# A four-layer graph attention kernel: normalised rows transposed by DMA in 16-bit halves in place of TensorE

## The chip, the cores and the metric

The kernel runs on one core of a Trainium2 chip. The metric is the device time of one execution in microseconds (us). Before the change three runs gave 2533.28 to 2535.13 us, median 2533.68.

## The reference

Four layers work on x (16 batches, 1024 nodes, 256 features, float32) and one adjacency matrix (1024 x 1024). Each layer normalises, projects, forms attention weights between all pairs of nodes, takes the weighted mean of the projected rows, and adds it to x:

```
h = max(layernorm(x), 0)
q = h @ W                                   # layers 0, 2: four heads of 64; layers 1, 3: one head of 256
e = leaky_relu(q @ a_src [i] + q @ a_dst [j])   # slope 0.2, in layer 3 0.01
attn = softmax over j of (e where adj, else -inf)
x = x + elu(attn @ q)                       # layer 3: relu in place of elu
```

Layers 0, 1 and 3 mask by adj > 0, layer 2 by adj != 0. Everything is float32.

## The kernel before

**Steps.** A step is one layer of one batch, 64 in all. Four batches are in work at a time (`STREAMS`), and `order_of_steps` interleaves them so that, but for the first few and the last, four-head and one-head steps alternate. A one-head step comes three places after the four-head step of the same batch, whose result it normalises; a four-head step comes five places after the one-head step before it, or starts a new batch.

**The main loop.** A step's work on TensorE is eight groups, each followed by an eviction (`aggregate`, L367 to L394). In a four-head step a group is half a head, 64-column pieces of the weight matrix as stationary operand and 65 moving columns; in a one-head step a group is one block of 128 rows with 257 columns. The last column carries the softmax denominator. ScalarE copies each group from its PSUM bank to `y` (L394). There are four such banks, shared with the projections and transposes. VectorE makes the weight tiles w (L363), one of 128 x 1024 for each head and block of 128 nodes, 32 in a four-head and 8 in a one-head step, into 18 buffers (`WBUFS`). The factor g that they read is broadcast over the partitions by a DMA (L346) and copied to PSUM by ScalarE (L358).

**The end of a step** (`finish`, L400 to L447) runs during the first groups of the next step: VectorE takes the reciprocal (L415), GpSimd scales (L425), ScalarE takes the exponential (L431), VectorE forms the ELU (L437) and GpSimd adds to x (L438).

**Preparation of a step** (`preparation`, L226) runs two to three steps ahead and is cut into 21 pieces: statistics on VectorE for each half of the nodes (L238), ten small operations on GpSimd that make the inverse deviation and the shift (L265 to L277; once for each half in a one-head step, once for both in a four-head step), normalisation of a half on ScalarE in four instructions (L283), two `transpose` pieces a half (eight TensorE transposes of 128 x 128 into a bank for each pair of halves and feature blocks, four a piece, evicted with Relu into `hT`, L291 and L292), four `project` pieces a half (two accumulating products each, L302, evicted by ScalarE, L304; after the fourth, two exponentials, L310 and L312, and a product on GpSimd, L314), and the factors and rows for g (L320 to L330).

**Order.** Nothing is scheduled by a program: each engine works in the order in which the code issues. A tuple of 21 numbers for each kind of step (`FOUR`, `ONE`, `SOON`, ...) says after which group each piece is issued, counted from the start of the step two places earlier. In the usual alternation `FOUR` and `ONE` apply. Pieces of two steps that fall on the same group are issued in the order of the steps. All ordinary DMAs go through SyncE's queue, in order too.

Of the kernel before, what the change touches and what calls it, by code (L numbers as in the profile page):

```python
# [26 lines left out]
F32 = mybir.dt.float32  # L27
BF16 = mybir.dt.bfloat16
I32 = mybir.dt.int32
U8 = mybir.dt.uint8  # L30
AF = mybir.ActivationFunctionType
ALU = mybir.AluOpType
AX = mybir.AxisListType
# [2 lines left out]
P = 128  # L36
EPS = 1e-5
SHIFT = 60.0
STREAMS = 4
WBUFS = 18  # L40

# [1 line left out]

FOUR = (-8, -8, -5, -3, -2, -1, -1, 0, 0, 0, 0, 0, 0, 2, 2, 2, 2, 3, 8, 8, 10)
SHORT = (-4, -4, -4, -2, -2, -1, -1, 0, 0, 0, 0, 0, 0, 2, 2, 2, 2, 3, 8, 8, 10)
ONE = (2, 2, 2, 4, 4, 5, 5, 6, 6, 6, 6, 6, 6, 8, 8, 8, 8, 8, 10, 10, 12)  # L50
SOON = (0, 0, 0, 1, 2, 3, 3, 4, 4, 5, 5, 5, 5, 6, 6, 7, 7, 7, 8, 8, 10)
FIRST = (-4, -4, -4, -2, -0.9, -1, -1, -0.8, -0.8, -0.8, -0.8, 0, 0, 1, 1, 1, 1, 1, 2, 2, 4)
TIGHT = (4, 4, 4, 6, 6, 7, 7, 8, 8, 8, 8, 8, 8, 9, 9, 9, 9, 9, 10, 10, 12)
LATE = (0, 0, 0, 1, 1, 2, 2, 3, 3, 3, 3, 3, 3, 4, 4, 4, 4, 5, 6, 6, 8)


LAYERS = [
# [8 lines left out]
def kernel(ctx: ExitStack, tc: tile.TileContext, x, adj, ws, avs, out):  # L66
    nc = tc.nc
    B, N, F = x.shape
    C = N // P
    K = F // P  # L70
    HALF = C // 2
# [3 lines left out]
    ident = const.tile([P, P], F32, name="ident")  # L75
# [8 lines left out]

    masks = [const.tile([P, C, N], U8, name=f"mask{i}") for i in range(2)]
    wx = []
# [11 lines left out]
    prep = ctx.enter_context(tc.tile_pool(name="prep", bufs=2))  # L98
# [9 lines left out]
    xs = {}  # L108
    state = [dict() for _ in steps]

    def bank(*shape):
        t = ps.tile([P, 512], F32, name="bank")
        n = math.prod(shape)
        if len(shape) == 1:
            return t[:, 0:n]
        names = "abc"[:len(shape)]
        return t[:, 0:n].rearrange(f"p ({' '.join(names)}) -> p {' '.join(names)}",
                                   **dict(zip(names, shape)))

    def heads_of(t, H):  # L120


        return t[..., 0:F + H].rearrange("p c (h d) -> p c h d", h=H)
# [7 lines left out]
    def weight_columns(l):  # L131
# [13 lines left out]
        def spread():  # L145
# [38 lines left out]
    def mask_rows(c):  # L184
# [3 lines left out]
        def fetch_rows():  # L188
            st["raw"] = work.tile([P, N], I32, name="w", bufs=WBUFS)
            nc.sync.dma_start(out=st["raw"], in_=adj.rearrange("(p c) j -> p c j", p=P)[:, c])  # L190

        def sign():
            st["sgn"] = work.tile([P, 2, N], BF16, name="w", bufs=WBUFS)
            nc.vector.tensor_scalar(st["sgn"][:, 0], st["raw"], -1.0, 1.0, op0=ALU.max,
                                    op1=ALU.min)
# [18 lines left out]
        def nonzero():  # L214
            nc.scalar.activation(masks[1][:, :, c * P:(c + 1) * P], st["pm"], AF.Square)

# [9 lines left out]
    def preparation(n):  # L226

        b, l = steps[n]
        H, slope, _, _ = LAYERS[l]
        D = F // H  # L230
        st = state[n]

        def stats(half):
            if half == 0:
                st["bn"] = small.tile([P, C, 6], F32, name="bn")
            bn = st["bn"]
            for c in range(half * HALF, (half + 1) * HALF):
                nc.vector.bn_stats(bn[:, c, :], xs[b][:, c, :])  # L238
            q = slice(half * HALF, (half + 1) * HALF)
            if n == 0:  # L240
                if half == 1:
                    combine_end(slice(0, HALF), nc.vector)
                combine(q, nc.vector)
            elif H == 1:

                combine(q, nc.gpsimd)
                combine_end(q, nc.gpsimd)
# [29 lines left out]
            engine.tensor_scalar(shift, shift, -0.5, None, op0=ALU.mult)  # L277

        def normalise(half):
            xn = st["xn", half] = prep.tile([P, HALF, F], F32, name="xn")  # L280
            for q in range(HALF):
                c = half * HALF + q
                nc.scalar.activation(xn[:, q, :], xs[b][:, c, :], AF.Identity,  # L283
                                     bias=st["shift"][:, c:c + 1], scale=st["rstd"][:, c:c + 1])

        def transpose(half, k):
            if k == 0:
                st["hT", half] = prep.tile([P, K, HALF * P], F32, name="hT")
            pt = bank(HALF, P)
            for q in range(HALF):  # L290
                nc.tensor.transpose(pt[:, q, :], st["xn", half][:, q, k * P:(k + 1) * P], ident)  # L291
            nc.scalar.activation(st["hT", half][:, k, :], pt.rearrange("p q i -> p (q i)"),  # L292
                                 AF.Relu)

        def project(c):
            if c == 0:
# [4 lines left out]
            for k in range(K):  # L301
                nc.tensor.matmul(pw, lhsT=st["hT", half][:, k, q * P:(q + 1) * P],  # L302
                                 rhs=wx[l][:, k, :], start=(k == 0), stop=(k == K - 1))
            nc.scalar.activation(st["whx"][:, c, :], pw, AF.Copy)  # L304
            if q < HALF - 1:
# [3 lines left out]
            wh = heads_of(st["whx"], H)[:, s]  # L309
            nc.scalar.activation(st["rcol"][:, s], wh[:, :, :, D], AF.Exp, bias=rbias[l],  # L310
                                 scale=1.0 - slope)
# [11 lines left out]
        def rows():  # L323
# [6 lines left out]
            nc.sync.dma_start(out=st["grow"].rearrange("h c i -> c h i"), in_=gT)  # L330

        out = [lambda: stats(0), lambda: stats(1), combine_all, lambda: normalise(0), lambda: normalise(1)]
        for half in range(2):
            out += [lambda half=half, k=k: transpose(half, k) for k in range(K)]
            out += [lambda c=c: project(c) for c in range(half * HALF, (half + 1) * HALF)]
# [24 lines left out]
    def weights(n, h, jc):  # L360

        w = state[n]["w", h, jc] = work.tile([P, N], F32, name="w", bufs=WBUFS)
        nc.vector.scalar_tensor_tensor(w, state[n]["g", h], state[n]["rcol"][:, jc, h:h + 1],  # L363
# [113 lines left out]
    def plan(n):  # L477
        new = preparation(n)
        agenda.extend((at, n, piece, i == len(new) - 1) for i, (at, piece) in enumerate(new))
        agenda.sort(key=lambda a: a[:2])  # L480
# [11 lines left out]
    def emit_heads(i):  # L492

        while done["g"] <= min(i + C // 2, done["tiles"] + C, len(tiles) - 1):
            n, h, _ = tiles[done["g"]]
            if n >= done["prepared"]:
                break
            broadcast(n, h)
            done["g"] += C
            fetch_heads()  # L500
# [12 lines left out]
    last, agenda_of = {}, []  # L513
    for n, (b, l) in enumerate(steps):

        free = -99
        if b % STREAMS in last:
            over = last[b % STREAMS] + 1
            free = 8 * over + (8 if l == 0 else 2 if LAYERS[steps[over][1]][0] == 1 else 4)
        last[b % STREAMS] = n  # L520
        start = 8 * (n - 2)
        kind = ONE if LAYERS[l][0] == 1 else SOON if n < 5 else FOUR
        if kind is FOUR and free > start + kind[0]:
            kind = SHORT
        if kind is ONE and free > start + kind[0]:
            kind = TIGHT
        if free > start + kind[0]:
            kind = LATE
            start = max(free, agenda_of[-1][0] + 5, start - LATE[7])
        agenda_of.append([start + k for k in kind] if n > 1 else FIRST)  # L530
        if n > 2:

            assert agenda_of[n][7] >= 8 * (n - 2)
            was = agenda_of[n - 1]
            assert agenda_of[n][3] >= was[5] and agenda_of[n][4] >= was[11]
    ending = []
    later = {}
    with tc.manual_schedule():
# [12 lines left out]
        nc.vector.tensor_copy(identb, ident)  # L551
        layer[0][1]()
        first = [piece for _, piece in preparation(0)]

        order = (
# [28 lines left out]
        for n in range(len(steps)):  # L584
            for k, (h, i0, per) in enumerate(groups(n)):
# [8 lines left out]
                while ending and ending[0][0] <= k:  # L594
                    ending.pop(0)[1]()
                upto = min(done["tiles"] + (6 if per > 1 else 3), done["free"] + WBUFS)
                emit_heads(upto - 1)
# [42 lines left out]
```

## Time and profile before

| what | value |
|---|---|
| median of three runs | 2533.68 us |
| profiled span | 2536.3 us |
| L379, aggregation on TensorE | 36,864 instructions, 1903.4 us busy |
| L302, projections on TensorE | 2,048 instructions, 481.5 us busy |
| L291, transposes on TensorE | 1,024 instructions, 136.8 us busy |
| L292, their evictions on ScalarE | 256, mean 585 ns |
| L283, normalisation on ScalarE | 512, mean 590 ns |
| L363, weight tiles on VectorE | 1,280, mean 1273 ns |
| L346, broadcast of a row by DMA | 159 of 512 KB |
| mean DMA rate over the span | 51 GB/s |

Busy time is the sum of an engine's instructions; matmuls are pipelined and their ends are modelled, so that the busy times on TensorE overlap a little. The chain is the work that ended last, followed back from the last instruction to whatever released it at each step; its shares say what a saved microsecond may be worth. A line of the timeline gives start, length, engine, line, operation, what it writes and reads, shapes and count, and in brackets the idle time ahead of it with what ended that time. PEld is TensorE's weight load, SPq the instructions that issue DMAs on SyncE.

### The profile page before, as it was taken

To read this page: it belongs to the slowest core of one execution; us is meant where nothing else is said; L and a number is where in the kernel's file an instruction comes from. 1 tells how busy PE (TensorE), PEld (TensorE's weight loads), DVE (VectorE), ACT (ScalarE), POOL (GpSimd) and SP (SyncE) were. 2 spreads that over 40 slices of the span, in tenths; PEclk is the share of its full clock that TensorE was granted. 3 is DMA by queue.
4 is the path that set the end of the run, shared out by engine and by line. 5 is a ranking of instruction groups with operands and counts; after the bars stand their busy time and mean duration, and the time that the engine had idled before them with its cause. 6 is when DMAs were issued, how large, how long until landed. Compare 5 with 4: busy or idle time off the path is not lost.

```text
span 2536.3 us, 88187 instructions
## 1 busy us (share of the span) xinstructions
PE 2489.7 (98%) x40096; PEld 2254.8 (89%) x40096; DVE 2014.6 (79%) x2138; ACT 1128.9 (45%) x2501; POOL 1106.6 (44%) x1366
## 2 busy tenths in 40 slices
PE   7999999999999999999999999999999999999999
PEld 6888898999988999988899899999889899899888
DVE  8988487888877987877888778878779887787973
ACT  6344455443454444544334544444444345544341
POOL 3345455443244554444332545543443345454351
PEclk9999999999999999999999999999999999999999
DMA  4201001122111111011221111111112201011101
GB/s 175 70 11 44 20 34 42 37 77 77 44 64 48 44 44 32 23 60 52 77 77 44 44 35 44 44 35 53 60 52 77 77 11 43 36 43 44 53 18 59
DMA packets 36847, 128.48 MB, mean 51 GB/s; under 512 B 6262, under 2 KB 9078, under 8 KB 34552
## 3 DMA queue, kind: packets, MB, share of 16 engines
q1 hardware_dynamic: 36462, 122.84, 13.8%
q8 instruction: 314, 5.14, 0.8%
q14 instruction: 61, 0.50, 0.1%
q10 hardware_dynamic: 10, 0.00, 0.0%
HBM read 105.39 MB, written 17.43 MB: 48 GB/s over the span
## 4 chain that ended last, share of the span: by engine, by line
PE 87%; DVE 7%; POOL 3%; issue 2%; ACT 1%; DMA 0%; DVEq 0%; SPq 0%; POOLq 0%; ACTq 0%
PE bank L379 65%; PE bank L302 17%; DVE w L363 5%; PE bank L291 4%; ACT xn L283 1%; POOL x L438 1%; DVE bn L238 1%; POOL rstd L271 1%; DVE e L437 0%; PE bank L326 0%; DVE e L424 0%; DVE wx L158 0%; DVE mask L211 0%; POOL shift L277 0%; DVE e L157 0%
## 5 line engine op out<-in xcount | busy, mean ns | idle before, releaser
L379 PE MATMUL bank<-whx,w 128*64 128x65 f32 x36864 | 1903.4, 241 | 20.9 <-issue 10.3
L379 PEld LDWEIGHTS bank<-whx,w 128*64 128x64 f32 x36864 | 1741.9, 144 | 162.8 <-issue 20.9
L363 DVE SCALAR_TENSOR_TENSOR w<-g,rcol,mask 128x1024 f32<-128x1024 f32 x1280 | 1540.6, 1273 | 359.2 <-PE bank L379 318.1
L394 ACT ACTIVATE y<-bank 128x260 f32<-128x260 f32 (+1 forms) x504 | 194.3, 386 | 1091.0 <-PE bank L379 1091.0
L425 POOL TENSOR_TENSOR y<-y,r 128x1024 f32<-128x1024 f32 x126 | 261.4, 2084 | 588.5 <-DVE e L424 435.1
L314 POOL TENSOR_TENSOR whx<-whx 128x1024 f32<-128x1024 f32 x128 | 259.2, 2025 | 561.9 <-ACT whx L312 561.9
L302 PE MATMUL bank<-wx,hT 128*128 128x264 f32 (+1 forms) x2048 | 481.5, 388 | 4.4 <-ACT y L394 3.9
L302 PEld LDWEIGHTS bank<-wx,hT 128*128 128x128 f32 x2048 | 382.4, 190 | 74.1 <-ACT y L394 13.1
L438 POOL TENSOR_TENSOR x<-x,e 128x1024 f32<-128x1024 f32 x96 | 246.0, 2572 | 144.9 <-DVE e L437 144.9
L283 ACT ACTIVATE xn<-x,shift,rstd 128x256 f32<-128x256 f32 x512 | 264.7, 590 | 72.9 <-POOL shift L277 70.9
L304 ACT ACTIVATE whx<-bank 128x264 f32<-128x264 f32 (+1 forms) x512 | 189.3, 385 | 178.4 <-PE bank L302 178.1
L238 DVE BATCH_NORM_STATS2 bn<-x 128x6 f32<-128x256 f32 x512 | 175.9, 411 | 77.2 <-POOL x L438 74.2
L437 DVE SCALAR_TENSOR_TENSOR e<-e,y 128x1024 f32<-128x1024 f32 x96 | 156.1, 1644 | 31.9 <-ACT e L431 22.8
L358 ACT ACTIVATE g<-gs 128x1024 f32<-128x1024 f32 x159 | 162.5, 1022 | 10.6 <-DVE w L363 7.8
L291 PE MATMUL bank<-ident,xn 128*128 128x128 f32 x1024 | 136.8, 275 | 7.6 <-ACT xn L283 7.4
L291 PEld LDWEIGHTS bank<-ident,xn 128*128 128x128 f32 x1024 | 119.8, 142 | 24.6 <-ACT xn L283 11.3
L292 ACT ACTIVATE hT<-bank 128x512 f32<-128x512 f32 x256 | 136.9, 585 | 1.1 <-PE bank L291 1.0
L271 POOL TENSOR_TENSOR rstd<-rstd,neghalf 128x4 f32<-128x4 f32 (+1 forms) x97 | 120.2, 1239 | 14.8 <-DVE shift L272 7.4
L431 ACT ACTIVATE e<-e 128x1024 f32<-128x1024 f32 x96 | 100.7, 1049 | 2.0 <-POOL e L427 1.7
L424 DVE SCALAR_TENSOR_TENSOR e<-y,r 128x1024 f32<-128x1024 f32 x58 | 68.5, 1222 | 2.1
L440 DVE SCALAR_TENSOR_TENSOR x<-y,x 128x1024 f32<-128x1024 f32 x30 | 43.3, 1444 | 10.0 <-POOL y L425 10.0
L312 ACT ACTIVATE whx<-whx,nbias 128x16 f32<-128x16 f32 (+1 forms) x128 | 40.2, 314 | 4.2
(65 smaller groups left out, 441.5 us busy)
## 6 DMA issues: line engine op xcount, KB each, us to landing
gs<-grow SPq DMA_DIRECT2D x159, 512.0 KB
x<-in_x SPq DMA_DIRECT2D x15, 1024.0 KB
out<-x SPq DMA_DIRECT2D x30, 512.0 KB
w<-in_adj SPq DMA_DIRECT2D x8, 512.0 KB
x<-in_x SPq DMA_DIRECT2D x2, 512.0 KB
wx<-in_L_gnn_W SPq DMA_DIRECT2D x8, 128.0 KB
out<-x SPq DMA_DIRECT2D x8, 128.0 KB
grow<-gT SPq DMA_DIRECT2D x32, 16.0 KB
```

Of the source, the lines that this page charges most:

```text
L238: nc.vector.bn_stats(bn[:, c, :], xs[b][:, c, :])
L283: nc.scalar.activation(xn[:, q, :], xs[b][:, c, :], AF.Identity, bias=st["shift"][:, c:c + 1], scale=st["rstd"][:, c:c + 1])
L291: nc.tensor.transpose(pt[:, q, :], st["xn", half][:, q, k * P:(k + 1) * P], ident)
L302: nc.tensor.matmul(pw, lhsT=st["hT", half][:, k, q * P:(q + 1) * P], rhs=wx[l][:, k, :], start=(k == 0), stop=(k == K - 1))
L304: nc.scalar.activation(st["whx"][:, c, :], pw, AF.Copy)
L314: nc.gpsimd.tensor_tensor(wh[:, :, :, 0:D], wh[:, :, :, 0:D], wh[:, :, :, D:D + 1].to_broadcast([P, HALF, H, D]), op=ALU.mult)
L358: nc.scalar.activation(g, state[n]["gs", h], AF.Copy)
L363: nc.vector.scalar_tensor_tensor(w, state[n]["g", h], state[n]["rcol"][:, jc, h:h + 1], masks[LAYERS[steps[n][1]][3]][:, jc, :], op0=ALU.m ...
L379: nc.tensor.matmul(acc[o % P:o % P + cols, q, :], lhsT=st["w", h, jc][:, o:o + cols], rhs=st["whx"][:, jc, h * (D + 1):(h + 1) * (D + 1)], ...
L394: nc.scalar.activation(st["y"][:, i0:i0 + per, h, :], acc, AF.Copy)
L425: nc.gpsimd.tensor_tensor(yh, yh, rb, op=ALU.mult)
L438: nc.gpsimd.tensor_add(xh, xh, e)
```

## The change

From the third step on, the normalised rows are transposed by the DMA engines. [...]GpSimd copies the lower and the upper 16 bits of a half's rows into two contiguous planes (`split`), one DMA on SyncE's queue transposes the sixteen 128 x 128 blocks of both planes, and ScalarE interleaves the two planes again while copying them to `hT` (`merge`). The integers pass through unchanged. `split` takes the place of the first `transpose` piece of a half and `merge` that of the second. Relu is applied by the normalisation. The aim is to free TensorE of the transposes and PSUM of their banks.

The four arrays of this path (normalised rows, planes, transposed planes, `hT`) share five buffers of 4 KB a partition (`HBUFS`), and the weight tiles give one up (`WBUFS` 17). The tuples move: in `FOUR` both normalisations and the first split come after the last group of the step before, the second split one group later, the merges one group after each other behind those, and all eight projections after one and the same group, the fourth of a step, where they stood in two pieces; in `ONE` splits and merges are two groups apart, the first four projections move from group 7 to group 8 of the step, and the rows for g come one group later.

```diff
-WBUFS = 18
+WBUFS = 17
+HBUFS = 5
-FOUR = (-8, -8, -5, -3, -2, -1, -1, 0, 0, 0, 0, 0, 0, 2, 2, 2, 2, 3, 8, 8, 10)
-SHORT = (-4, -4, -4, -2, -2, -1, -1, 0, 0, 0, 0, 0, 0, 2, 2, 2, 2, 3, 8, 8, 10)
-ONE = (2, 2, 2, 4, 4, 5, 5, 6, 6, 6, 6, 6, 6, 8, 8, 8, 8, 8, 10, 10, 12)
-SOON = (0, 0, 0, 1, 2, 3, 3, 4, 4, 5, 5, 5, 5, 6, 6, 7, 7, 7, 8, 8, 10)
+FOUR = (-8, -8, -5, -1, -1, -1, 1, 3, 3, 3, 3, 0, 2, 3, 3, 3, 3, 4, 8, 8, 10)
+SHORT = (-4, -4, -4, -1, -1, -1, 1, 3, 3, 3, 3, 0, 2, 3, 3, 3, 3, 4, 8, 8, 10)
+ONE = (2, 2, 2, 4, 5, 4, 6, 7, 7, 7, 7, 5, 7, 8, 8, 8, 8, 8, 11, 11, 12)
+SOON = (0, 0, 0, 1, 2, 1, 3, 4, 4, 5, 5, 2, 5, 6, 6, 7, 7, 7, 8, 8, 10)
-TIGHT = (4, 4, 4, 6, 6, 7, 7, 8, 8, 8, 8, 8, 8, 9, 9, 9, 9, 9, 10, 10, 12)
-LATE = (0, 0, 0, 1, 1, 2, 2, 3, 3, 3, 3, 3, 3, 4, 4, 4, 4, 5, 6, 6, 8)
+TIGHT = (4, 4, 4, 5, 6, 5, 7, 8, 8, 8, 8, 6, 8, 9, 9, 9, 9, 9, 10, 10, 12)
+LATE = (0, 0, 0, 1, 2, 1, 3, 4, 4, 4, 4, 2, 4, 5, 5, 5, 5, 5, 6, 6, 8)
...
         def normalise(half):
-            xn = st["xn", half] = prep.tile([P, HALF, F], F32, name="xn")
+            xn = st["xn", half] = prep.tile([P, K, HALF, P], F32, name="rows", bufs=HBUFS)
             for q in range(HALF):
                 c = half * HALF + q
-                nc.scalar.activation(xn[:, q, :], xs[b][:, c, :], AF.Identity,
+                nc.scalar.activation(xn[:, :, q, :],
+                                     xs[b][:, c, :].rearrange("p (k i) -> p k i", k=K), AF.Relu,
                                      bias=st["shift"][:, c:c + 1], scale=st["rstd"][:, c:c + 1])
+        def split(half):
+            xn = st["xn", half].rearrange("p k q i -> p (k q i)").bitcast(U16)
+            bits = prep.tile([P, 2, K * HALF * P], U16, name="rows", bufs=HBUFS)
+            nc.gpsimd.tensor_copy(bits.rearrange("p s n -> p n s"),
+                                  xn.rearrange("p (n s) -> p n s", s=2))
+            st["turned", half] = prep.tile([P, 2, K * HALF, P], U16, name="rows", bufs=HBUFS)
+            nc.sync.dma_start_transpose(
+                out=st["turned", half].rearrange("p s n i -> p (s n) i"),
+                in_=bits.rearrange("p s n -> p (s n)"))
+        def merge(half):
+            st["hT", half] = prep.tile([P, K, HALF * P], F32, name="rows", bufs=HBUFS)
+            nc.scalar.activation(
+                st["hT", half].rearrange("p k i -> p (k i)").bitcast(U16).rearrange(
+                    "p (n s) -> p n s", s=2),
+                st["turned", half].rearrange("p s n i -> p (n i) s"), AF.Copy)
         def transpose(half, k):
+            if n > 1:
+                (merge if k else split)(half)
+                return
...
-            assert agenda_of[n][3] >= was[5] and agenda_of[n][4] >= was[11]
+            assert agenda_of[n][3] >= agenda_of[n - 1][12]
```

More of the change, by code (lines that the diff above doesn't have):

```diff
@@ L30 @@
 U8 = mybir.dt.uint8
+U16 = mybir.dt.uint16
 AF = mybir.ActivationFunctionType
@@ L279, in normalise @@
         def normalise(half):
-            xn = st["xn", half] = prep.tile([P, HALF, F], F32, name="xn")
+            xn = st["xn", half] = prep.tile([P, K, HALF, P], F32, name="rows", bufs=HBUFS)
             for q in range(HALF):
                 c = half * HALF + q
-                nc.scalar.activation(xn[:, q, :], xs[b][:, c, :], AF.Identity,
+                nc.scalar.activation(xn[:, :, q, :],
+                                     xs[b][:, c, :].rearrange("p (k i) -> p k i", k=K), AF.Relu,
                                      bias=st["shift"][:, c:c + 1], scale=st["rstd"][:, c:c + 1])
+        def split(half):
[13 more added lines that the diff above has]
+                st["turned", half].rearrange("p s n i -> p (n i) s"), AF.Copy)
         def transpose(half, k):
+            if n > 1:
+                (merge if k else split)(half)
+                return
             if k == 0:
-                st["hT", half] = prep.tile([P, K, HALF * P], F32, name="hT")
+                st["hT", half] = prep.tile([P, K, HALF * P], F32, name="rows", bufs=HBUFS)
             pt = bank(HALF, P)
             for q in range(HALF):
-                nc.tensor.transpose(pt[:, q, :], st["xn", half][:, q, k * P:(k + 1) * P], ident)
+                nc.tensor.transpose(pt[:, q, :], st["xn", half][:, k, q, :], ident)
             nc.scalar.activation(st["hT", half][:, k, :], pt.rearrange("p q i -> p (q i)"),
-                                 AF.Relu)
+                                 AF.Copy)
         def project(c):
@@ L533 @@
             assert agenda_of[n][7] >= 8 * (n - 2)
-            was = agenda_of[n - 1]
-            assert agenda_of[n][3] >= was[5] and agenda_of[n][4] >= was[11]
+            assert agenda_of[n][3] >= agenda_of[n - 1][12]
     ending = []
```

## The prediction

> **What bounds the kernel now.** I read the page's busy shares and its chain first, then windows over equal stretches, then the order of time inside one of them.
>
> ```profile
> PE 2489.7 (98%) x40096; PEld 2254.8 (89%) x40096; DVE 2014.6 (79%) x2138; ACT 1128.9 (45%) x2501; POOL 1106.6 (44%) x1366
> ...
> PE bank L379 65%; PE bank L302 17%; DVE w L363 5%; PE bank L291 4%; ACT xn L283 1%; POOL x L438 1%; DVE bn L238 1%; POOL rstd L271 1%; DVE e L437 0%; PE bank L326 0%; DVE e L424 0%; DVE wx L158 0%; DVE mask L211 0%; POOL shift L277 0%; DVE e L157 0%
> ```
>
> TensorE carries 87% of the chain. The transposes of L291, which the change takes away, hold 4% of it.
>
> ```profile
> 881.50:958.20 76.70, 76.67 (x1253) 69.71 (x1252) 61.48 (x65) 35.81 (x80) 38.43 (x44) 1.00 0.11 37
> 958.20:1035.00 76.80, 76.76 (x1253) 69.80 (x1254) 61.58 (x65) 35.97 (x80) 38.47 (x45) 1.00 0.11 37
> ```
>
> Length, then busy time of TensorE, its weight loads, VectorE, ScalarE, GpSimd. From about 500 us on, a pair of steps (one of four heads, one of one head) repeats every 76.7 us, and TensorE has no gap. So its sum sets the pair, as long as what a projection needs is there in time. The timeline of one pair shows how close that is:
>
> ```profile
> 923.79 0.39 ACT L394 ACTIVATE y<-bank 128x260 f32<-128x260 f32 x1 [3.34 <-PE bank L379]
> ...
> 932.79 5.58 POOL L438 TENSOR_TENSOR x<-x,e 128x1024 f32<-128x1024 f32 x2 [1.16 <-DVE e L437]
> ...
> 941.61 0.23 POOL L277 TENSOR_SCALAR shift<-shift 128x4 f32<-128x4 f32 x1
> ...
> 941.88 2.08 ACT L283 ACTIVATE xn<-x,shift,rstd 128x256 f32<-128x256 f32 x4
> ...
> 944.53 1.01 PEld L291 LDWEIGHTS bank<-ident,xn 128*128 128x128 f32 x8
> ...
> 945.08 0.23 POOL L277 TENSOR_SCALAR shift<-shift 128x4 f32<-128x4 f32 x1
> ...
> 945.50 3.34 PEld L379 LDWEIGHTS bank<-whx,w 128*128 128x128 f32 x16
> ...
> 949.09 3.94 PE L302 MATMUL bank<-wx,hT 128*128 128x258 f32 x16
> 949.23 0.24 POOL L277 TENSOR_SCALAR shift<-shift 128x8 f32<-128x8 f32 x1
> ```
>
> TensorE ends a four-head step at 923.7. Its result passes through the division, ELU and residual (x ready at 938.4), the statistics and GpSimd's small operations; ScalarE normalises the first half for the next one-head step at 941.88, TensorE transposes it at 944.53 and projects at 949.09. Meanwhile GpSimd works through three sets of small operations one behind the other: first half (ends 941.84), second half (945.31), and those of the following four-head step (949.47). ScalarE's normalisation waited for GpSimd here: no slack worth speaking of lies in this latency.
>
> [...] here eight blocks took TensorE 0.97 us from first load to the next work (944.53 to 945.50), so 121 ns each[...], and no run yet shows a DMA transpose. [...] here only writes stride, and L427's 1040 ns for 1,024 elements (in order, one input) shows 1.02 ns an element. [...]
>
> **The change part by part.**
>
> *Taken from TensorE.* Four sets of eight transposes a pair. From first weight load to the next work's first load they took 1.18, 0.97, 0.98 and 1.18 us (892.29, 944.53, 952.66, 957.01): 4.3 us a pair, over 31 pairs 134 us. (The chain's 4% is 104 us, a lower reading.) The first two steps keep TensorE.
>
> *ScalarE.* Relu moves into the normalisation: same instruction, nothing. Four evictions of 585 ns a step become two merges of 2,048 elements[...]. A pair: 7.6 in place of 4.7 us; 35.8 becomes 38.7 of 76: its sum costs nothing, its place does, below.
>
> *GpSimd.* Four copies of 2,048 16-bit elements a pair. Lower bound by L427: 2,048 x 1.02 = 2.1 us. [...] I take 2.1. The sum, 38.4 + 8.4, hides under 76.
>
> *The DMA.* 512 KB, SBUF to SBUF. The nearest row is one broadcast row load of the same size:
>
> ```profile
> 935.84 0.32 SPq L346 DMA_DIRECT2D gs<-grow  x1
> ```
>
> Windows of 1 us around it show its data moving from 936.9 to about 938.5: 1.1 us before the first byte, about 2.6 in all. That is the lower bound. [...] 4.4 us, which I take. [...] Four a pair add 2 MB to some 2.8: no bandwidth limit.
>
> *The new wait.* In the changed program's order ScalarE's first merge stands between the evictions of one-head groups 7 and 8 of the pair, and TensorE's first projections follow group 8. The first split stands on GpSimd behind all three sets of small operations. So, in the clock of the trace above: sets end 949.47, split 951.6, transpose landed 956.0, merged 957.9; with three hand-overs of 0.1, hT is there at 958.2. TensorE, with no transposes in between, has done its eight one-head groups (spacing of evictions 3.66, then 3.48) at 923.7 + 28.0 = 951.7. It stands still 6.5 us. Behind the waiting merge ScalarE holds group 8's eviction, which a spare PSUM bank covers, and, after the projections, the second merge and eight normalisations (1.9 + 4.2 us) ahead of the next eviction. TensorE's four banks fill in that time: three of the second four projections fit, the fourth and the next group wait; about 1 us (0 to 1.5). Who waits for TensorE is everything: this latency starts at the end of one four-head step and ends in the projection ahead of the next, so it comes once a pair and cannot be made up.
>
> *Projections in one piece, moved transposes, fewer buffers.* The eight four-head projections follow the fourth group of that step, some 20 us after their normalisation; splits, transposes and merges of 2.1, 4.4 and 1.9 fit beside three groups and four projections: nothing. One weight buffer less (17): the seven tiles ahead of the reciprocal wait for the sixth four-head group, which ends 7.5 us ahead of the step's end; 7 x 1.27 = 8.9 us put the reciprocal 1.4 us after it, where it is now (925.19): nothing. The "rows" buffers, five shared by four uses, make the third split and fourth transpose wait for projections that lie before them anyway.
>
> *Sum.* 6.5 + 1.0 - 4.3 = +3.2 us a pair; about 30 pairs (start and end are unlike the rest): +96 us, 2,630.
>
> **The rivals.** (a) The preparation is hidden and TensorE keeps its gain: 2,534 - 134 = 2,400. For it: TensorE has no gap now and all other sums fit. Against: it needs hT 6.5 us earlier than I find, and even with the lower bounds (2.1 + 2.6 + 1.9) the wait is 4.7, more than the 4.3 gained. It would take a faster path to 949.47 too. Partial forms lie between 2,400 and 2,528. (b) All at its lower bound, no bank wait: +0.4 a pair, 2,546. (c) The split pays for its strided writes[...], 2,735. For it: writes of 2 bytes, alternating; against: no row shows a stride costing GpSimd (L314 and L425 take some 2.0 us for two inputs). (d) Transposes near 20 us: the wait is 23, four in a row on one queue fill the pair, 3,100 or more. Against: the same-size load at 2.6.
>
> **How the numbers follow.** Main case 0.45; (a) 0.14; (b) 0.12, part of it within 0.2%; (c) 0.22; (d) 0.07. Faster 0.14, same 0.03, slower 0.83. The range leaves out most of (a) and all of (d): from 2,500, a partial gain, to 2,790, a slow split with a transpose of 6 us.
>
> **What would show it.** Right: TensorE idle some 6 us once a pair ahead of the first one-head projection, released by ScalarE's merge, which waits for a DMA; pair of about 80 us; split near 2.1 us, merge near 1.9, transpose landing in 3 to 5. Wrong: TensorE still without a gap and a pair near 72.5; GpSimd's split starting ahead of the third set; a landing under 2 us or over 6; gaps ahead of the four-head projections instead.

## The result, and the profile after

The changed kernel takes 3392.44 us (median; 3391.62 to 3394.06) beside 2533.48 us for the kernel before: 1.339 times as long, 95% interval 1.337 to 1.342. The forecast of 2630 us had the direction and fell short by 762 us; the range ended at 2790.

First the busy shares and the chain of waits of the changed kernel (shares of the span by engine, then by line):

```profile
PE 2569.0 (76%) x39104; PEld 2254.8 (66%) x39104; DVE 2214.6 (65%) x2138; ACT 1253.8 (37%) x2377; POOL 2223.0 (66%) x1490
...
POOL 40%; PE 33%; DMA 8%; ACT 7%; issue 6%; DVE 5%; POOLq 0%; DVEq 0%; ACTq 0%
```

TensorE fell from 98% to 76% busy, and its share of the chain from 87% to 33%. GpSimd doubled its busy time (1106.6 to 2223.0 us) and holds 40% of the chain. At 66% busy it is not the bound by its sum: with 2,223 us of work it could end far earlier. It is the bound by where its work stands. The groups of instructions say which work (busy time, mean ns of one | idle time ahead of it on its engine, and its releaser):

```profile
L328 PE MATMUL bank<-wx,rows 128*128 128x264 f32 (+1 forms) x2048 | 658.5, 487 | 772.2 <-ACT rows L303 459.1
L294 POOL COPY rows<-rows 128x2048 uint16<-128x2048 uint16 x124 | 1164.5, 9496 | 86.6 <-ACT rows L285 86.5
...
L303 ACT ACTIVATE rows<-rows 128x2048 uint16<-128x2048 uint16 x124 | 265.9, 2145 | 665.1 <-DMA rows<-rows 647.7
```

One split (L294) takes 9.5 us where the prediction priced 2.1. The merge (L303) takes 2.1 us and stood 648 us waiting for the DMA; the projections (L328) stood 772 us and themselves became slower, 487 ns in place of 388. Before the change they stood 4.4 us:

```profile
L302 PE MATMUL bank<-wx,hT 128*128 128x264 f32 (+1 forms) x2048 | 481.5, 388 | 4.4 <-ACT y L394 3.9
```

One of the two gaps in a pair of steps, ahead of the first one-head projection, in the timeline (start, length, engine, line, ..., in brackets the idle time ahead and what ended it):

```profile
1564.26 0.24 POOL L279 TENSOR_SCALAR shift<-shift 128x8 f32<-128x8 f32 x1
1564.45 18.29 POOL L294 COPY rows<-rows 128x2048 uint16<-128x2048 uint16 x2
1573.73 29.27 SPq L297 DMA_TRANSPOSE rows<-rows  x3
1578.15 2.15 ACT L303 ACTIVATE rows<-rows 128x2048 uint16<-128x2048 uint16 x1 [13.61 <-DMA rows<-rows]
...
1580.35 5.81 PEld L328 LDWEIGHTS bank<-wx,rows 128*128 128x128 f32 x16 [13.15 <-ACT rows L303]
1580.35 6.21 PE L328 MATMUL bank<-wx,rows 128*128 128x258 f32 x16 [12.75 <-ACT rows L303]
```

This is the predicted sequence link for link: the third set of small operations ends (1564.5), the split follows it, then the DMA, the merge, the projection. The transpose is issued at 1573.73 and its data is merged from 1578.15 on, 4.4 us later, as forecast; the merge takes 2.15 for 1.9. Only the split differs: of the two in the 18.29 us, the first ends as the DMA is issued, 9.3 us after its start.

The other gap was not forecast. It stands ahead of and within the projections of four heads:

```profile
1485.94 9.41 POOL L294 COPY rows<-rows 128x2048 uint16<-128x2048 uint16 x1 [2.15 <-ACT rows L285]
...
1496.91 1.91 POOL L340 TENSOR_TENSOR whx<-whx 128x1024 f32<-128x1024 f32 x1
1498.75 9.28 POOL L294 COPY rows<-rows 128x2048 uint16<-128x2048 uint16 x1
...
1502.59 2.05 PE L328 MATMUL bank<-wx,rows 128*128 128x264 f32 x8 [1.64 <-ACT rows L303]
...
1512.38 2.15 ACT L303 ACTIVATE rows<-rows 128x2048 uint16<-128x2048 uint16 x1 [9.57 <-DMA rows<-rows]
1514.43 0.37 ACT L420 ACTIVATE y<-bank 128x260 f32<-128x260 f32 x1
...
1514.85 8.39 PE L328 MATMUL bank<-wx,rows 128*128 128x264 f32 x24 [10.21 <-ACT y L420]
```

The two splits of this step stand one behind the other on GpSimd with two multiplications between them; the second ends at 1508.0, its merge at 1514.5. TensorE projects the first half after 1.6 us of waiting and then stands 10.2 us (in some other pairs 2.7 and 7.6). The releaser named is the eviction L420, but that eviction only stood on ScalarE behind the second merge, which waited for the DMA: the split is the cause here too.

Last, windows of the changed kernel (length; busy time of TensorE, its weight loads, VectorE, ScalarE, GpSimd; then the granted TensorE clock, the share of the DMA engines, GB/s): a whole pair of steps, the first projections after the gap at 1580, and the aggregation after them.

```profile
1474.48:1580.35 105.87, 79.60 (x1219) 69.93 (x1219) 70.89 (x64) 37.99 (x74) 66.82 (x45) 0.87 0.26 66
...
1580.30:1582.00 1.70, 1.65 (x4) 1.37 (x5) 1.40 (x3) 0.27 (x1) 1.70 (x1) 0.50 0.00 0
1582.00:1584.00 2.00, 2.00 (x7) 1.54 (x6) 2.00 (x2) 0.39 (x1) 0.74 (x1) 0.50 0.01 2
...
1586.50:1590.30 3.80, 3.80 (x129) 3.80 (x128) 0.00 (x0) 3.63 (x6) 1.90 (x1) 1.00 0.03 5
```

A pair takes 105.9 us in place of 76.7. After the two long gaps TensorE comes back at half clock: sixteen one-head projections take 6.2 us here and 3.75 in runs below without a long gap. The granted clock was 0.50 at 1514.9 to 1519 and 1.00 from 1521 after the one, 0.50 at 1580.3 to 1584 and 1.00 at 1586.5 after the other: the full clock came back some 5 us after the work did. In other pairs of this run gaps of 1.9 to 2.7 us were followed by the half clock too (0.50 at 1609.6 to 1612.5 behind 2.7 us; eight four-head projections took 3.1 to 3.7 us in place of 2.05).

The pair's 29.2 us, then: gaps of 12.75, 1.64, 10.21 and 0.7 us (the last a wait for a bank), 25.3 together; half clock 6.2 - 3.75 = 2.5 after one gap and about 2.9 after the other (24 four-head projections in 8.4 us beside 5.5 at full clock), 5.4 together; transposes -4.3. That makes 26.4; the other 2.8 is about 1 us of smaller gaps and 1.8 of longer busy time that I did not trace one by one.

### The profile page after: what moved, and what is told of

It reads as the page before. It is cut to its first block, busy times and chain, and to the rows that moved or that the text cites. A ratio compares the mean times of both kernels' runs of the same rounds, so it can differ in the third digit from the quotient of the medians.

```text
span 3391.2 us, 86617 instructions
## 1 busy us (share of the span) xinstructions
PE 2569.0 (76%) x39104; PEld 2254.8 (66%) x39104; DVE 2214.6 (65%) x2138; ACT 1253.8 (37%) x2377; POOL 2223.0 (66%) x1490
## 4 chain that ended last, share of the span: by engine, by line
POOL 40%; PE 33%; DMA 8%; ACT 7%; issue 6%; DVE 5%; POOLq 0%; DVEq 0%; ACTq 0%
POOL rows L294 26%; PE bank L405 21%; PE bank L328 12%; DMA rows<-rows 8%; ACT rows L303 3%; POOL rstd L273 3%; DVE e L463 2%; POOL x L464 2%; DVE w L389 2%; ACT rows L285 2%; POOL whx L340 2%; POOL y L451 2%; ACT e L457 1%; POOL rstd L271 1%; POOL rstd L270 1%
## 5 line engine op out<-in xcount | busy, mean ns | idle before, releaser
L405 PE MATMUL bank<-whx,w 128*64 128x65 f32 x36864 | 1893.5, 241 | 29.1 <-DVE w L389 22.7
L328 PE MATMUL bank<-wx,rows 128*128 128x264 f32 (+1 forms) x2048 | 658.5, 487 | 772.2 <-ACT rows L303 459.1
L294 POOL COPY rows<-rows 128x2048 uint16<-128x2048 uint16 x124 | 1164.5, 9496 | 86.6 <-ACT rows L285 86.5
L328 PEld LDWEIGHTS bank<-wx,rows 128*128 128x128 f32 x2048 | 489.3, 247 | 919.7 <-ACT rows L303 478.2
L420 ACT ACTIVATE y<-bank 128x260 f32<-128x260 f32 (+1 forms) x504 | 193.1, 383 | 881.9 <-PE bank L405 881.9
L303 ACT ACTIVATE rows<-rows 128x2048 uint16<-128x2048 uint16 x124 | 265.9, 2145 | 665.1 <-DMA rows<-rows 647.7
L463 DVE SCALAR_TENSOR_TENSOR e<-e,y 128x1024 f32<-128x1024 f32 x96 | 222.2, 2316 | 209.5 <-ACT e L457 177.0
L464 POOL TENSOR_TENSOR x<-x,e 128x1024 f32<-128x1024 f32 x96 | 227.5, 2370 | 96.1 <-DVE e L463 96.1
L285 ACT ACTIVATE rows<-x,shift,rstd 128x256 f32<-128x256 f32 x512 | 261.3, 588 | 8.8 <-POOL shift L279 7.0
L441 DVE RECIPROCAL r<-y 128x32 f32<-128x32 f32 (+1 forms) x63 | 17.5, 278 | 312.4 <-ACT y L420 310.1
L466 DVE SCALAR_TENSOR_TENSOR x<-y,x 128x1024 f32<-128x1024 f32 x30 | 127.5, 4249 | 16.2 <-POOL y L451 16.2
L450 DVE SCALAR_TENSOR_TENSOR e<-y,r 128x1024 f32<-128x1024 f32 x58 | 87.1, 1543 | 2.1
```

Source lines behind the costliest of these rows:

```text
L285: nc.scalar.activation(xn[:, :, q, :], xs[b][:, c, :].rearrange("p (k i) -> p k i", k=K), AF.Relu, bias=st["shift"][:, c:c + 1], scale=st[ ...
L294: nc.gpsimd.tensor_copy(bits.rearrange("p s n -> p n s"), xn.rearrange("p (n s) -> p n s", s=2))
L303: nc.scalar.activation(st["hT", half].rearrange("p k i -> p (k i)").bitcast(U16).rearrange("p (n s) -> p n s", s=2), st["turned", half].re ...
L405: nc.tensor.matmul(acc[o % P:o % P + cols, q, :], lhsT=st["w", h, jc][:, o:o + cols], rhs=st["whx"][:, jc, h * (D + 1):(h + 1) * (D + 1)], ...
L420: nc.scalar.activation(st["y"][:, i0:i0 + per, h, :], acc, AF.Copy)
L463: nc.vector.scalar_tensor_tensor(e, e, -1.0, yh, op0=ALU.add, op1=ALU.max)
```

## The experiments

All ratios are to the kernel before, timed on the same chip (its medians there are 2532.6 to 2534.3 us). Two theories were in dispute at first. The first: the split is slow because its instruction walks element by element, so that its 2-byte writes jump between the two planes 2 KB apart, and all the rest of the excess follows from it. Its rival: the order of the pieces or the fewer buffers cost the time.

**e1_order: the same split, walked plane by plane.** The same bits go to the same places; only the order differs: all lower halves, then all upper halves.

```diff
-            nc.gpsimd.tensor_copy(bits.rearrange("p s n -> p n s"),
-                                  xn.rearrange("p (n s) -> p n s", s=2))
+            nc.gpsimd.tensor_copy(bits, xn.rearrange("p (n s) -> p s n", s=2))
```

> The changed kernel, but GpSimd's split walks plane after plane (writes contiguous, reads every second 16-bit element) in place of element after element (each write 2 KB away from the last). Theory 'write order': the split costs about 2.1 us (2,048 x 1.02 ns) in place of 9.4, the first one-head projection is waited for some 6 us a pair in place of 13, VectorE's two-input operations are no longer held, and the whole takes about 2,630 us (my first sum, with its other terms as they measured). Rival '16-bit elements': a 16-bit element costs GpSimd 4.6 ns in whatever order, the split stays at 9.4 and the time near 3,390. Rival 'transpose DMA': if the DMA and not the split were the cause the time stays over 3,000 even with a short split.

Measured: 2692.8 us, 1.063 (1.061 to 1.065). The group of the split in this run:

```profile
L294 POOL COPY rows<-rows 128x2048 uint16<-128x2048 uint16 x124 | 234.8, 1906 | 84.8 <-ACT rows L285 84.6
```

The split fell from 9496 to 1906 ns, and 700 of the 859 us lost were gone. What is left, 159 us, is more than the forecast's 96 but has its form: one long gap a pair, ahead of the first one-head projection, in the timeline

```profile
1509.46 2.14 ACT L302 ACTIVATE rows<-rows 128x2048 uint16<-128x2048 uint16 x1 [6.37 <-DMA rows<-rows]
...
1511.65 6.60 PE L327 MATMUL bank<-wx,rows 128*128 128x258 f32 x16 [5.51 <-ACT rows L302]
```

of 5.5 us (forecast 6.5), with a pair of 82.7 us (forecast 79.9). The sixteen projections behind it take 6.60 us, not 3.75: the half clock (0.50 at 1511.7 to 1516), which the forecast did not have. It cost 2.9 us here and 1.4 to 2.9 in the other pairs; over the whole run the projections were busy 62 us longer than before, about 2 a pair.

**e2_forms: the copies by themselves.** The kernel before, with nine forms of copy of one half's rows added at its very end, three of each; their results are not used.

```diff
+            nc.gpsimd.tensor_copy(d.rearrange("p s n -> p n s"), pairs16)   # L612
+            nc.gpsimd.tensor_copy(d, planes)                                # L613
+            nc.gpsimd.tensor_copy(d.rearrange("p s n -> p (s n)"), src)     # L614
...
+            nc.scalar.activation(d, planes, AF.Copy)                        # L617
+            nc.scalar.activation(d.rearrange("p s n -> p n s"), pairs16, AF.Copy)  # L618
...
+            nc.vector.tensor_copy(d.rearrange("p s n -> p n s"), pairs16)   # L620
```

> The kernel before, with a measurement of copies behind its last step, alone on their engines: on GpSimd 2,048 16-bit elements with alternating writes (as in the split), plane by plane, contiguous, half of them (1,024) plane by plane, and 1,024 float32 contiguous; plane by plane and alternating also on ScalarE and VectorE. Theory 'write order': 9.4, then about 2.1, 2.1, 1.1 and 1.04 us on GpSimd. Rival '16-bit elements': 9.4, 9.4, 9.4, 4.7 and 1.04. ScalarE about 1.9 to 2.15 either way; VectorE about 2.2 or less.

Measured, in the groups of that run (means of three; GpSimd's and VectorE's copies overlap in part, and GpSimd's copy of 1,024 float32, L616, took 1.1 us ahead of VectorE's first and 5.9 to 6.0 the other times, so the means of those two are upper readings; ScalarE's lie within 8 ns):

```profile
L612 POOL COPY xn<-x 128x2048 uint16<-128x2048 uint16 x3 | 28.6, 9522 | 6.6 <-DVE x L391 6.6
L618 ACT ACTIVATE xn<-x 128x2048 uint16<-128x2048 uint16 x3 | 27.7, 9230 | 0.1
L620 DVE COPY xn<-x 128x2048 uint16<-128x2048 uint16 x3 | 17.3, 5756 | 0.1
L614 POOL COPY xn<-x 128x2048 uint16<-128x2048 uint16 x3 | 5.8, 1920 | 0.2
L617 ACT ACTIVATE xn<-x 128x2048 uint16<-128x2048 uint16 x3 | 5.7, 1910 | 51.1 <-POOL xn L616 51.1
L613 POOL COPY xn<-x 128x2048 uint16<-128x2048 uint16 x3 | 5.7, 1896 | 0.2
```

GpSimd needs 1920 ns for a plain contiguous copy of 2,048 16-bit elements, 1896 plane by plane, which reads every second element, and 9522 with alternating writes. So this stride of the reads, 4 bytes, costs nothing and the alternation of the writes everything; the rival falls, as 16-bit elements in order are cheap. ScalarE shows the same two prices, 1910 and 9230, so this is not a peculiarity of GpSimd; VectorE took 5.3 to 6.0 us for alternating writes. Both were expected to be cheap either way, and were not. Which part of the alternation costs, the 2 KB between two writes or single elements of 2 bytes, no run varied. The whole run, 2593.8 us, says no more, as the copies lengthen it.

**e3_sched: the order and the buffers alone.** The changed kernel's tuples, weight buffers and "rows" buffers, but from the third step on TensorE transposes as before, both pieces where the merge stands.

```diff
-                (merge if k else split)(half)
+                if k:
+                    turn_block(half, 0)
+                    turn_block(half, 1)
                 return
```

(`turn_block` is the old body with eight transposes and two evictions.)

> The changed kernel with its order, its 17 weight buffers and its five shared row buffers, but TensorE transposes as before, both sets of a half where the changed kernel has its merge; no split, no DMA. Theory 'the path through GpSimd and DMA is the cause': within 1% of the kernel before (2,534), as TensorE has its old sum and finds its rows ready. Rival 'order and buffers': clearly slower, by as much of the 859 us as they cause.

Measured: 2551.95 us, 1.007 (1.006 to 1.009). The rival falls: moving the pieces and giving up a weight buffer costs 18 us, not hundreds. "Nothing", as the prediction had it, was nearly right. Without split and transposed planes the five "rows" buffers have only two uses here, not four; that four uses do not cost hundreds either shows in e9_merge_first, which has all four and takes 2490 us.

**e4_act: the split on ScalarE.** If GpSimd's row of three sets, splits and multiplications is what makes the latency, taking the split from it should close the gap.

```diff
-            nc.gpsimd.tensor_copy(bits.rearrange("p s n -> p n s"),
-                                  xn.rearrange("p (n s) -> p n s", s=2))
+            nc.scalar.activation(bits, xn.rearrange("p (n s) -> p s n", s=2), AF.Copy)
```

> The changed kernel with the split on ScalarE (plane by plane) right behind the normalisation, so that it waits neither for GpSimd's small operations nor costs GpSimd anything. Theory 'latency of the path': split 1.9 to 2.15 us, transpose 4.4, merge 2.15 after the normalisation: the first projection is waited for about 1 us, ScalarE's longer rows of work ahead of the evictions cost some 3 us a pair, the transposes save 4.3: about 2,500, between 2,440 and 2,560. Rival 'transpose DMA': still over 2,700, as the DMA stays.

Measured: 2583.22 us, 1.020 (1.018 to 1.021), above what was expected. The gap did close, to 0.4 to 0.9 us, and sixteen projections took 3.75 us. But a new wait came: after the projections ScalarE works through the second merge, eight normalisations and now a split, and the eviction that frees a bank stands behind them. In the timeline:

```profile
1534.63 1.64 PE L327 MATMUL bank<-wx,rows 128*128 128x258 f32 x4 [2.50 <-ACT y L419]
1536.19 12.84 PE L404 MATMUL bank<-whx,w 128*64 128x65 f32 x384
```

The prediction's bank wait, put at 1.0 us there, grew to 2.5, and over the whole run TensorE's projections waited 73 us for that eviction (23 in e1_order). This wait too brought the half clock: 0.50 from 1536.2 to 1538, and the four projections took 1.64 us in place of 1.14, the 384 aggregation products behind them 12.84 in place of 11.42.

**e6_combine: the third set of small operations behind the split.** e1_order, and in `FOUR` the piece of the four-head step's small operations moves three groups later, so that GpSimd splits first.

```diff
-FOUR = (-8, -8, -5, -1, -1, -1, 1, 3, 3, 3, 3, 0, 2, 3, 3, 3, 3, 4, 8, 8, 10)
+FOUR = (-8, -8, -2, -1, -1, -1, 1, 3, 3, 3, 3, 0, 2, 3, 3, 3, 3, 4, 8, 8, 10)
```

> e1_order, and GpSimd's small operations for the following four-head step (4.2 us) issued three groups later, behind both one-head splits. Theory 'latency from the end of the four-head step to the one-head projection': the split starts 4.2 us earlier, the wait of 5.5 us ahead of the first projection falls to about 1.3, and the half-clock projections behind it (6.6 in place of 3.7 us) go with it: about 6.5 us a pair, 2,693 - 30 x 6.5 = 2,500. Rival 'bank wait': the time goes instead to the wait of the second projections on ScalarE's normalisations and falls by less than 60.

Measured: 2540.1 us, 1.003 (1.001 to 1.005): 153 us off e1_order for one number, though short of the 2500 expected. The gap fell from 5.5 to 1.4 us, and with it the half clock went (1.00 at 1503.9 to 1507.6):

```profile
1503.85 3.75 PE L327 MATMUL bank<-wx,rows 128*128 128x258 f32 x16 [1.43 <-ACT rows L302]
```

Three pairs kept it, behind gaps of 2.7 to 4.4 us. The run shows that this latency is worth more than its length (4.1 us less of gap, 5 us less a pair), and that the third set was in it, as the prediction's clock of the trace had it.

**e7_later: one-head merges and projections one group later.** e6_combine, with the remaining 1.4 us covered by one more aggregation group of 3.5 us; the preparation of the four-head step also moves one group later (its tuples `FOUR` and `SHORT` are not shown here; `FOUR` stands under e10_norms_later).

```diff
-ONE = (2, 2, 2, 4, 5, 4, 6, 7, 7, 7, 7, 5, 7, 8, 8, 8, 8, 8, 11, 11, 12)
+ONE = (2, 2, 2, 4, 5, 4, 7, 8, 8, 8, 8, 5, 8, 8, 8, 8, 8, 8, 11, 11, 12)
```

> e6_combine, and all eight one-head projections one group later (behind the first four-head group), merges and normalisations of the four-head step moved behind them with the order of the buffers kept. Theory 'latency': no wait is left ahead of either projection, TensorE keeps most of the 4.3 us a pair that the transposes gave: 2,410 to 2,470, faster than both. Rival 'contention': TensorE has the room but something else, ScalarE's longer rows of work or VectorE with 17 buffers, takes its place: 2,500 or more.

Measured: 2634.14 us, 1.040 (1.038 to 1.042), a clear miss. Now both halves are projected one behind the other, and the second merge was issued after the first half's evictions on ScalarE, so TensorE waited for it between the two halves:

```profile
1560.46 5.44 PE L327 MATMUL bank<-wx,rows 128*128 128x258 f32 x16 [3.17 <-ACT rows L302]
```

That is 3.2 us, and 5.44 in place of 3.75 us for the next sixteen projections, over which the granted clock fell to 0.50.

**e8_nodma: e1_order without the DMA.** The transposition is left out of the computation: the merge joins GpSimd's untransposed planes, so the projections multiply rows that were not transposed. All else is as in e1_order.

```diff
-            st["turned", half] = prep.tile([P, 2, K * HALF, P], U16, name="rows", bufs=HBUFS)
-            nc.sync.dma_start_transpose(
-                out=st["turned", half].rearrange("p s n i -> p (s n) i"),
-                in_=bits.rearrange("p s n -> p (s n)"))
+            st["turned", half] = bits.rearrange("p s (n i) -> p s n i", i=P)
```

> e1_order without the transposing DMA: merge reads GpSimd's planes themselves, so the rows stay untransposed (left out: the transposition). It shows what the DMA's latency is worth in the changed order. Theory 'latency': 4.4 us less on the path, the wait of 5.5 us falls to about 1.1 and the half-clock stretch goes: some 7 us a pair, about 2,480, close to e6_combine, which takes away about as much of the path elsewhere. Rival 'the DMA is hidden': no change from 2,693.

Measured: 2492.55 us, 0.984 (0.983 to 0.986), as expected. In this order the DMA's 4.4 us are worth 200 us: without them no long gap is left. TensorE's waits for the merge (us in total, times, longest; 153.2, 32 and 5.7 in e1_order):

```profile
PE bank L324 <- ACT rows L299: 27.0, 27, 1.4
```

The run also takes one of four uses from the "rows" buffers. That it is the latency that costs, not the traffic or the buffers, shows in e9_merge_first below, which has both and takes as long as this run; by the changed kernel's page this DMA queue took 21% of the DMA engines' time.

**e9_merge_first: e7_later with the second merge ahead of the first half's projections.** One number against e7_later, which fixes the order in which ScalarE meets the merge and the evictions.

```diff
-ONE = (2, 2, 2, 4, 5, 4, 7, 8, 8, 8, 8, 5, 8, 8, 8, 8, 8, 8, 11, 11, 12)
+ONE = (2, 2, 2, 4, 5, 4, 7, 8, 8, 8, 8, 5, 7.5, 8, 8, 8, 8, 8, 11, 11, 12)
```

> e7_later with the second one-head merge ahead of the projections on ScalarE in place of behind the first four's evictions. In e7_later TensorE waited 3.2 us for that merge and then ran its projections at half clock (5.4 in place of 3.7 us). Theory 'e7_later lost its time to that wait': some 5 us a pair come back, about 2,485. Rival 'VectorE': both projections behind one four-head group leave VectorE without free weight buffers for 11.7 us a pair, so that TensorE then waits for weight tiles: over 2,560.

Measured: 2490.27 us, 0.983 (0.981 to 0.984): the expected value, and faster than both kernels, with the DMA transposes in it. Its busy shares and its projections in the groups:

```profile
PE 2407.0 (97%) x39104; PEld 2157.1 (87%) x39104; DVE 2044.0 (82%) x2138; ACT 1249.3 (50%) x2377; POOL 1305.7 (52%) x1490
```

```profile
L327 PE MATMUL bank<-wx,rows 128*128 128x264 f32 (+1 forms) x2048 | 488.2, 393 | 17.0 <-ACT rows L302 10.4 <-ACT y L419 4.5 <-ACT whx L329 0.2
```

TensorE is 97% busy again, the projections waited 17 us in the whole run in place of 772, and all 32 of a one-head step run in one piece (7.56 us).

**e10_norms_later and e11_set_later: is the order of ScalarE's normalisations enough?** e10_norms_later is e6_combine with only the four-head tuples of e7_later (everything after the small operations one group later; `SHORT`, not shown, moves likewise). e11_set_later adds to it that the second half's statistics and small operations come 2.5 groups later.

```diff
-FOUR = (-8, -8, -2, -1, -1, -1, 1, 3, 3, 3, 3, 0, 2, 3, 3, 3, 3, 4, 8, 8, 10)
+FOUR = (-8, -8, -2, 0, 0, 0, 2, 4, 4, 4, 4, 1, 3, 4, 4, 4, 4, 5, 8, 8, 10)
...
-ONE = (2, 2, 2, 4, 5, 4, 6, 7, 7, 7, 7, 5, 7, 8, 8, 8, 8, 8, 11, 11, 12)
+ONE = (2, 4.5, 4.5, 4, 5, 4, 6, 7, 7, 7, 7, 5, 7, 8, 8, 8, 8, 8, 11, 11, 12)
```

> e6_combine with the four-head step's normalisations issued behind the second one-head projections, so that ScalarE has no row of 6 us ahead of the first four-head eviction (four-head merges and projections one group later). Theory 'bank wait': the 1.3 us a pair that the second projections waited are gone, 2,540 - 40 = 2,500. Rival 'VectorE': its tiles come later against TensorE as the projections move, no gain or slower.

Measured: 2521.69 us, 0.995 (0.994 to 0.997), 18 us less than e6_combine where 40 were expected. The waits of the projections for the eviction `y` fell from 23.8 to 4.5 us: the bank wait came from the normalisations ahead of that eviction. Of the 53 us of waits for the merge 46 stayed.

> e10_norms_later, and the second half's statistics and small operations of the one-head step issued behind the first split. Theory 'latency': the first split starts up to 1.3 us earlier, which is what is left of the wait ahead of the first projection: some 40 less than e10_norms_later, about 2,460, faster than both kernels. Rival: the second half's transpose becomes the late one, no gain.

Measured: 2697.47 us, 1.064 (1.062 to 1.066), a miss by 240 us. The second half's statistics now came behind nine weight tiles on VectorE (10.8 us), and the second normalisation waited for them on ScalarE with the first merge behind it. In the timeline:

```profile
1507.91 2.07 ACT L285 ACTIVATE rows<-x,shift,rstd 128x256 f32<-128x256 f32 x4 [6.80 <-POOL shift L279]
...
1512.34 6.02 PE L327 MATMUL bank<-wx,rows 128*128 128x258 f32 x16 [4.70 <-ACT rows L302]
```

TensorE stood 4.7 us for that merge, and the half clock was back (0.50 at 1512.4 to 1515).

**All runs in one table.** Span, the projections' idle and busy time from the groups on TensorE, and what remains when both are taken from the span (us):

| kernel | span | projections: idle ahead | projections: busy | remainder |
|---|---|---|---|---|
| before | 2536.3 | 4.4 | 481.5 | 2050.4 |
| changed | 3391.2 | 772.2 | 658.5 | 1960.5 |
| e1_order | 2691.6 | 176.5 | 543.7 | 1971.4 |
| e3_sched | 2551.5 | 0.1 | 476.2 | 2075.2 |
| e4_act | 2581.9 | 93.6 | 496.8 | 1991.5 |
| e6_combine | 2543.9 | 76.8 | 499.8 | 1967.3 |
| e7_later | 2630.5 | 109.6 | 539.2 | 1981.7 |
| e8_nodma | 2489.6 | 46.0 | 485.7 | 1957.9 |
| e9_merge_first | 2487.1 | 17.0 | 488.2 | 1981.9 |
| e10_norms_later | 2519.4 | 51.0 | 491.3 | 1977.1 |
| e11_set_later | 2698.4 | 158.6 | 561.9 | 1977.9 |

The remainder of all kernels without TensorE's transposes lies within 1958 to 1992; the spans differ by 900 us. So what tells them apart is how long the projections wait and at what clock they then run (in e4_act a part of the half clock falls on the aggregation, and so into the remainder). The table also prices the gain: the remainder fell by 59 to 93 us against the kernel before, and by 84 to 117 us against e3_sched, which has the changed order and buffers and still transposes on TensorE. The prediction counted 134.

## Why the prediction was wrong

**The step that failed: GpSimd's "Four copies of 2,048 16-bit elements a pair", of which it says "I take 2.1".** Measured: 9.5 us, four and a half times as much. The 2.1 was a price for something else: L427 reads and writes in order (1040 ns for 1,024 elements). Here the reads ran in order too, and e2_forms shows that even a step of 4 bytes in them is free (1896 ns beside 1920); the writes alternated. The prediction saw "writes of 2 bytes, alternating" and that "no row shows a stride costing GpSimd", and took the lack of a row for a bound. No row wrote single elements in alternation, so nothing bounded it from above.

**What followed from it by the prediction's own sums.** Put 9.3 in place of 2.1 in "sets end 949.47, split 951.6": the wait of 6.5 becomes 13.7; 12.75 was measured. The mechanism held to the link, and the term was mis-sized. This alone does not give the whole loss: 13.7 + 1.0 - 4.3 = 10.4 us a pair would make about 2,850.

**A second step failed with it: "splits, transposes and merges of 2.1, 4.4 and 1.9 fit beside three groups and four projections: nothing".** With 9.4 us each and two multiplications between them, the two splits end 22 us after the first began, and TensorE stood 1.6 and 10.2 us. The prediction had named "gaps ahead of the four-head projections" as a sign against it. They came in addition to, not in place of, the gap that it forecast, and they are nearly half of the idle time of a pair. In e1_order, with 1.9 us splits, the waits were back to one gap and a bank wait of 0.7 us, as that step had it.

**A term that was missing: the clock.** A wait was priced at its own length. The gap of e1_order also cost 1.4 to 2.9 us of half clock behind it, about 2 a pair; in the changed kernel it was 5.4 in the pair shown. With 62 us for it the main case would have read 2692 beside 2692.8 measured for e1_order, a kernel whose split costs what the prediction assumed. That this fits so well is partly luck: the waits of the projections grew by 172 us there, where 30 x 7.5 = 225 were forecast, and the remainder fell by 79, where 30 x 4.3 = 129 were, and the two errors cancel.

**What held.** The direction and where the latency begins and ends; GpSimd's three sets ahead of the split (e6_combine: 153 us for moving one of them); the transpose at 4.4 us and the merge at 2.15 (4.4 and 1.9 forecast; no trace then showed either, and both were the author's estimates); the order and the buffers at nearly nothing (18 us); a bank wait of 0.7 to 1.3 (1.0). Against "pair of about 80 us" stand 105.9, and 82.7 in e1_order. One reading beside the path has to be put right: 121 ns is each transpose's share of eight that overlap on TensorE (0.97 us for the eight); a single one took 275 ns (L291, mean).

**The gain.** The 4.3 us a pair that TensorE sheds were counted as 134 us; the table shows 59 to 93. The prediction gave the chain's 104 as a lower reading, and set it aside. Part of the difference is not the transposes but the new order and the weight buffer, which the prediction put at nothing: e3_sched's remainder is 25 us above that of the kernel before, and measured from there the gain is 84 to 117. Weight tiles that come late are in it: TensorE's aggregation waited 8.8 us for them before, 22.2 in e3_sched and 29.8 in e9_merge_first. The rest I did not take apart.

**The rivals.** (c) named the right term, the alternating writes, but sized it with a price that no trace showed: 2,735, three quarters of the loss missing. (d) came near in time for a reason that did not occur. (a), the hidden preparation at 2,400, is what the change is for; its mechanism is real, as e9_merge_first shows with another order, but it gives 2490, as the gain is smaller than counted.

## What to carry to other kernels

When data is split into planes, look at the order in which an instruction writes, not only at its element count: let the destination run contiguously and the source stride (1.9 us in place of 9.5 here). A price that no row of the profile bounds from above needs a wide upper end, or a measurement, and a wait on TensorE has to be priced with the slow clock behind it (here from gaps of some 2 us on). Moving work off a saturated engine pays only when the latency that it adds is placed: here the same transposes by DMA cost 34% or gained 1.7%, by the order of one copy's writes and a few numbers in the tuples.

## What the runs showed of the hardware that was not expected

- A copy of 2,048 16-bit elements whose writes alternate between two places 2 KB apart took 9.2 to 9.5 us on GpSimd and 9.2 on ScalarE, 4.5 to 4.6 ns an element, beside 1.9 us (0.93 ns an element) for contiguous writes, whether the reads stride by 4 bytes or not. VectorE took 5.3 to 6.0, in part beside running GpSimd copies.
- The merge also writes in pairs of halves, but into one contiguous row, while its reads alternate between planes: 2.1 us. On ScalarE these alternating reads were cheap (2.1 us) where alternating writes were dear (9.2 us).
- A DMA transpose of sixteen blocks of 128 x 128 2-byte elements within SBUF took some 4.4 us: in the changed kernel 69 of the 93 merges that waited for one began 4.3 to 4.6 us after the end of their split, the others within 6.4 us.
- A VectorE operation with two inputs was held beside GpSimd's splits. In the changed kernel L466 took 8.8 us in all twelve cases that overlapped a split and 1.2 us in the eighteen others:

```profile
1604.58 9.28 POOL L294 COPY rows<-rows 128x2048 uint16<-128x2048 uint16 x1
1605.52 8.81 DVE L466 SCALAR_TENSOR_TENSOR x<-y,x 128x1024 f32<-128x1024 f32 x1
```

The two end within 0.5 us of each other. Its mean was 4249 ns, and with fast splits in e1_order it was 1215. No run separates what this alone cost; TensorE's aggregation waited 22.7 us for weight tiles from VectorE in both kernels.
- TensorE's clock behind a gap does not follow from the gap's length alone. Ahead of the projections, gaps of up to 1.75 us were followed by the full clock in every run (3.75 us for sixteen one-head projections), and gaps of 4.2 us or more by the half clock every time (5.1 to 6.8 us for sixteen, whatever the length, up to 12.8 us). In between it varied: behind the same gap of 3.17 us, thirty times in e7_later, sixteen took 3.75 us three times and 5.1 to 6.8 the other times. The half clock lasted 3 to 6 us in the stretches looked at (0.50 at 1511.7 to 1516 in e1_order, 0.67 to 1518.2, 1.00 from there).
